# Shifting features by one token: transfers between partitions in place of products with 0/1 matrices

## The chip, the cores and the metric

The kernel runs on one core of one Trainium2 chip. The metric is the device time of one execution in microseconds (us), as the median of several runs. The core has five queues of work of its own that run side by side and wait for one another on semaphores: TensorE (PE, matrix products, its weight loads shown as PEld), VectorE (DVE), ScalarE (ACT), GpSimd (POOL) and SyncE (SP), which here only issues DMA transfers.

## The reference

The input x has 2 sequences of 1024 tokens with 128 features. Four blocks follow one another: a full attention with 16 heads, two layers of local attention with a feed-forward part, a causal attention with rotary positions, and a mixture of 8 experts; after each of them x plus the result is normalized. The change touches the two local layers. Cut to what matters:

```python
def shift_token(t):
    t1, t2 = jnp.split(t, 2, axis=-1)
    t2 = jnp.pad(t2, ((0, 0), (1, 0), (0, 0)))[:, :-1]
    return jnp.concatenate([t1, t2], axis=-1)

def _layer(x, wqkv, qs, ksc, wo, lg, lb, w1, b1, w2, b2):
    h = shift_token(x)
    q, k, v = jnp.split(h @ wqkv, 3, axis=-1)        # 8 heads of 64
    ...                                              # norm of q and k, rotation, windows of 64
    x = x + o @ wo
    h = shift_token(x)                               # the shift of this change
    h = (h - h.mean(-1)) / jnp.sqrt(h.var(-1) + 1e-05) * lg + lb
    a, g = jnp.split(h @ w1 + b1, 2, axis=-1)
    return x + (a * jax.nn.gelu(g, approximate=False)) @ w2 + b2
```

Features 64 to 127 of a token are replaced by those of the token before it in its sequence; the first token of a sequence gets zeros.

## The kernel before

Tokens lie on the 128 partitions. A sequence has 8 tiles of 128 tokens; 4 of them make a half, and a block is a (layer, sequence b, half hf). Within a block, token p of tile t lies on partition p at place t, so a shift by one token is a shift by one partition, and partition 0 of a tile needs what partition 127 of the tile before it holds.

The local layers run as one loop of 36 steps over 32 tiles (16 for each layer), written out by hand in `local_layers`. In a step each of some dozen stages works on another tile: the projection on the newest, scores two tiles behind it, the softmax three, the outputs four, the output projection five (`add_out`), and the sum that makes x1, the input of the feed-forward part, six behind (`add_x`, L813 on DVE, at the start of the step). Between the stages stand named places, `early`, `turns`, `mid`, `post` and `late`, into which the feed-forward pieces of a block are put by step number. PE, ACT, DVE and POOL do their work strictly in the order written. SP is not in that order: its transfers are placed by a planner at compile time.

The x1 of block k is complete with the `add_x` of step R = 4k + 9, for k from 0 to 6 the steps 9, 13, 17, 21, 25, 29 and 33. In that step, in the place `late` at its end:

- `ff_shift` (L461 to L474) has PE write the shifted half into a PSUM bank: a product with a 0/1 matrix that moves every row by one (L465), a second that carries the last row of a tile to the next (L466), and, for the second half of a sequence, one with the row kept from the first half (L468, tile `last`, made by POOL at L473).
- `ff_stats` (L476 to L481) builds the tile h: POOL copies the features that stay (L479), DVE copies the shifted ones out of PSUM (L480), and then `norm_factors` takes statistics on DVE (L99, L101) and a power on POOL (L105, L106).

One step later `ff_norm` applies the factors in place (L118 on DVE) and `ff_turn` transposes h for the products with w1. The PSUM bank comes from `single`, a pool of two banks that the loop's other small results share.

Around them, in step R, DVE has the scores of the step (L740, L745, L748), the division (L787, L789), and then, after the statistics, the next step's sums of squares (L689) and rotation (L696). POOL has the power of the query and key norms (L690, L691), the scaling (L701), the rotation's second half (L658, two products), and, for the next step, a copy of keys (L720), for which the score products on PE (L732) wait. For the blocks of layer 1 the sum with the local layers' input (`last_sum`: L545 on POOL, L99 on DVE, L105 and L106 on POOL) of block k-1 stands in `late` of the same step, ahead of `ff_stats`. SP issues two transfers in each step, of 64 partitions by 2080 bytes each, which copy values to other partitions (vh from vb, L680 and L683).

An eighth block, the last, is done by the same functions in the next attention's loop (`second_attention`).

Of the kernel before, what the change touches and what calls it, by code (L numbers as in the profile page):

```python
# [7 lines left out]
F32 = mybir.dt.float32  # L8
# [4 lines left out]
P = 128  # L13
B = 2
T = 1024
D = 128
NBLK = 2
NT = 4
# [29 lines left out]
def transformer_kernel(ctx: ExitStack, tc: tile.TileContext, a, out):  # L48
    nc = tc.nc
# [3 lines left out]
    xp = ctx.enter_context(tc.tile_pool(name="x", bufs=3))  # L53
# [36 lines left out]
    def norm_tiles(n):  # L90
        return (
            sp.tile([P, n, 6], F32, tag="ln_st", name="ln_st"),
            sp.tile([P, n, 2], F32, tag="ln_mv", name="ln_mv"),
            sp.tile([P, n], F32, tag="ln_rs", name="ln_rs"),
        )

    def norm_stats(y, tiles, which):
        for i in which:
            nc.vector.bn_stats(tiles[0][:, i, :], y[:, i, :])  # L99
        for i in which:  # L100
            nc.vector.bn_aggr(tiles[1][:, i, :], tiles[0][:, i, :])  # L101

    def norm_power(tiles, n):
        _, mv, rs = tiles
        nc.gpsimd.tensor_scalar_add(rs, mv[:, :, 1], EPS)  # L105
        nc.gpsimd.tensor_tensor(rs, rs, neghalf.to_broadcast([P, n]), ALU.pow)  # L106
        return mv, rs

    def norm_factors(y, n):

        tiles = norm_tiles(n)
        norm_stats(y, tiles, range(n))
        return norm_power(tiles, n)

    def norm_apply(o, y, factors, which):
        mv, rs = factors
        for i in which:
            nc.vector.tensor_scalar(  # L118
                o[:, i, :], y[:, i, :], mv[:, i, 0:1], rs[:, i : i + 1], ALU.subtract, ALU.mult
            )  # L120
# [333 lines left out]
    def feed_forward(pool2, single, double, ws, x1s, lasts, mbufs=1, gbufs=2):  # L454

        ffs = {}
        ones = [pool2.tile([P, 512], F32, name=f"mt2_{n}") for n in range(mbufs)]
        for mt in ones:
            nc.gpsimd.memset(mt, 1.0)

        def ff_shift(layer, b, hf):  # L461
            x1 = x1s[layer, b, hf]

            sh = single("ps_sh")[:, :256].rearrange("p (t d) -> p t d", d=64)
            nc.tensor.matmul(sh, shift, x1[:, :, 64:128], start=True, stop=False)  # L465
            nc.tensor.matmul(sh[:, 1:4, :], carry, x1[:, 0:3, 64:128], start=False, stop=(hf == 0))  # L466
            if hf:
                nc.tensor.matmul(  # L468
                    sh[:, 0, :], carry, lasts[layer, b], start=False, stop=True
                )  # L470
            else:
                lasts[layer, b] = xp.tile([P, 64], F32, tag="last", name="last", bufs=2)
                nc.gpsimd.tensor_copy(lasts[layer, b], x1[:, 3, 64:128])  # L473
            ffs[layer, b, hf] = {"sh": sh}  # L474

        def ff_stats(layer, b, hf):  # L476
            x1, sh = x1s[layer, b, hf], ffs[layer, b, hf]["sh"]
            h = pool2.tile([P, NT, D], F32, tag="h", name="h", bufs=2)
            nc.gpsimd.tensor_copy(h[:, :, 0:64], x1[:, :, 0:64])  # L479
            nc.vector.tensor_copy(h[:, :, 64:128], sh)  # L480
            ffs[layer, b, hf] = {"h": h, "ln": norm_factors(h, NT)}  # L481

        def ff_norm(layer, b, hf):
            f = ffs[layer, b, hf]
            norm_apply(f["h"], f["h"], f["ln"], range(NT))

        def ff_turn(layer, b, hf):
            f, w = ffs[layer, b, hf], ws[layer]
            ps = single("ps_hn")
            transpose_tiles(ps, lambda i: f["h"][:, i, :], NT)  # L490
            hnT = pool2.tile([P, 512], F32, tag="hnT", name="hnT", bufs=mbufs)
            nc.scalar.activation(hnT, ps, AF.Identity, scale=w["lng"], bias=w["lnb"])
            f["hnT"], f["mts"] = hnT, []

        def ff_in(layer, b, hf, c):
            f, w = ffs[layer, b, hf], ws[layer]
            c0, m = CH[c]
            ps = double("ps_w1")
            for n in range(2):
                nc.tensor.matmul(  # L500
                    ps[:m, n * 512 : (n + 1) * 512],
                    w["w1"][:, n * HID + c0 : n * HID + c0 + m], f["hnT"], start=True, stop=True,
                )
            gl = pool2.tile([P, 512], F32, tag="gl", name="gl", bufs=gbufs)
            nc.scalar.activation(gl[:m], ps[:m, 512:], AF.Gelu, bias=w["b1"][:m, 1, c : c + 1])
            f["parts"] = f.get("parts", {})
            f["parts"][c] = ps, gl

        def ff_gate(layer, b, hf, c):
            f, w = ffs[layer, b, hf], ws[layer]  # L510
            m = CH[c][1]
            ps, gl = f["parts"].pop(c)
            if c == 2:
                mt = ones[0]
                ones.append(ones.pop(0))
            else:
                mt = pool2.tile([P, 512], F32, tag=f"mt{c}", name=f"mt{c}", bufs=mbufs)
            nc.vector.scalar_tensor_tensor(  # L518
                mt[:m], ps[:m, :512], w["b1"][:m, 0, c : c + 1], gl[:m], ALU.add, ALU.mult
            )  # L520
            f["mts"].append(mt)

        def ff_out(layer, b, hf):
            f, w = ffs[layer, b, hf], ws[layer]
            ps = single("ps_w2")
            for i in range(NT):
                for c, (c0, m) in enumerate(CH):
                    m += c == 2
                    nc.tensor.matmul(
                        ps[:, i * P : (i + 1) * P], f["mts"][c][:m, i * P : (i + 1) * P],  # L530
                        w["w2"][:m, c, :], start=(c == 0), stop=(c == 2),
                    )
            f["ps"] = ps

        def ff_add(layer, b, hf):
            f = ffs.pop((layer, b, hf))
            x2 = xp.tile([P, NT, D], F32, tag=f"x{b}{hf}", name=f"xf_{b}{hf}")
            nc.vector.tensor_add(x2, f["ps"].rearrange("p (t d) -> p t d", d=D), x1s[layer, b, hf])
            x[b, hf] = x2

        return ff_shift, ff_stats, ff_norm, ff_turn, ff_in, ff_gate, ff_out, ff_add

    def last_sum(x_in, b, hf):
        y = xp.tile([P, NT, D], F32, tag="y", bufs=2, name=f"yl{b}{hf}")
# [18 lines left out]
    def local_layers(ws, tab):  # L563
# [20 lines left out]
        hTs, x1s, lasts, st = {}, {}, {}, [{} for _ in range(N)]  # L584
# [251 lines left out]
        early, turns, mid, post, late = {}, {}, {}, {}, {}  # L836

        def at(when, step, f, *args):
            when.setdefault(step, []).append((f, args))
# [9 lines left out]
        def steps(p, p2, ps, finish):  # L849
            nonlocal pool, pool2, psl  # L850
            pool, pool2, psl = p, p2, ps
# [6 lines left out]
                vbufs.append(v)  # L858
            for n in range(VH):
                vhbufs.append(pool.tile([P, 8, 65], F32, name=f"vh{n}"))  # L860
            ff_shift, ff_stats, ff_norm, ff_turn, ff_in, ff_gate, ff_out, ff_add = feed_forward(
                pool2, single, double, ws, x1s, lasts
            )

# [1 line left out]
            for k in range(7):  # L866
                block = layer, b, hf = k // 4, k % 2, k // 2 % 2
                ready = 4 * k + 9
                at(late, ready, ff_shift, *block)
                at(late, ready, ff_stats, *block)  # L870
                at(early, ready + 1, ff_norm, *block)
                at(late, ready + 1, ff_turn, *block)
                at(late, ready + 2, ff_in, *block, 0)
                at(early, ready + 3, ff_gate, *block, 0)
                at(turns, ready + 3, ff_in, *block, 1)
                at(mid, ready + 3, ff_gate, *block, 1)
                at(mid, ready + 3, ff_in, *block, 2)
                at(post, ready + 3, ff_gate, *block, 2)
                at(turns, ready + 4, ff_out, *block)
                at(mid, ready + 4, ff_add, *block)  # L880
                if layer == 0:
                    at(turns, ready + 5, next_head, 1, b, hf)
                else:
                    at(late, ready + 4, sum_up, b, hf)
                    if hf == 0:
                        at(early, ready + 5, lambda b, hf: normed[b, hf](), b, hf)
# [66 lines left out]
    def second_attention(pool, pool2, poolf, single, double, route, wc, woc, cs, ws, left):  # L953
# [133 lines left out]
        def group(f, g, *args):  # L1087
# [2 lines left out]


        norm_before, x_in, x1s, lasts = left
        ff_shift, ff_stats, ff_norm, ff_turn, ff_in, ff_gate, ff_out, ff_add = feed_forward(
            poolf, single, double, ws, x1s, lasts, mbufs=2, gbufs=4
        )
        early, late, normed = {}, {}, {}

        def at(when, step, f, *args):
            when.setdefault(step, []).append((f, args))
# [8 lines left out]
        block = (1, 1, 1)  # L1108
# [533 lines left out]
    with (  # L1642
# [8 lines left out]
        def single(name):  # L1651
            return psc.tile([P, 512], F32, tag="s", bufs=4, name=name)
# [99 lines left out]
```

## Time and profile before

| what | value |
|---|---|
| median of 3 runs | 1082.17 us (1081.94 to 1082.19) |
| the profiled execution | 1082.95 us, of which 1081.2 us are its span |
| busy: PE, DVE, ACT, POOL | 986.3, 797.5, 746.6, 569.9 us |
| first `add_x` of a complete block to the last (steps 9 to 33) | 514.2 us to 791.9 us from the span's start |
| a cycle of four steps in between | 45.7 to 46.8 us |
| granted TensorE clock, mean | 0.97 |

The busy time of an engine is an average over stages with quite different limits, so the stage is read by itself: the timeline of each engine within one step R, and what each instruction there waited for.

### The profile page before, as it was taken

How to read it: one execution, taken by the hardware profiler on the slowest of the kernel's cores; microseconds unless marked ns; L12 is line 12 of the kernel's file. 1: busy time of each engine (PE TensorE's matmuls, PEld its weight loads, DVE VectorE, ACT ScalarE, POOL GpSimd, SP SyncE). 2: the span in 40 equal slices, each digit the busy share in tenths (PEclk: the TensorE clock that was granted, in tenths of full speed). 3: DMA queues.
4: the chain of work that ended last, by engine and by line, in shares of the span. 5: the costliest groups of instructions: out<-in, count | busy, mean ns of one | idle time of the engine just before them, and what ended most of it. 6: DMA issues, size and time to landing. Idle time of an engine off the chain costs nothing. (4 is left out here: it accounts for less than half of the span.)

```text
span 1081.2 us, 21885 instructions
## 1 busy us (share of the span) xinstructions
PE 986.3 (91%) x8091; PEld 579.3 (54%) x8091; DVE 797.5 (74%) x1676; ACT 746.6 (69%) x1508; POOL 569.9 (53%) x625
## 2 busy tenths in 40 slices
PE   9999999999999999779989999999787799999891
PEld 3433333334333332456666757666564466689891
DVE  5988888887998887778968777695754387757443
ACT  1488888888888887568878788797662565444442
POOL 4044333434433433779978687786723135418653
PEclk8999999999999999889999999999898899999996
DMA  3111434112120200201101001010000000146883
GB/s 92 33 38 50 125 86 107 23 57 65 55 55 14 79 2 2 74 21 32 26 16 26 22 17 31 21 31 21 16 2 1 0 1 23 42 162 211 310 296 126
DMA packets 57211, 65.09 MB, mean 60 GB/s; under 512 B 9077, under 2 KB 43425, under 8 KB 57105
## 3 DMA queue, kind: packets, MB, share of 16 engines
q1 hardware_dynamic: 53472, 57.40, 18.2%
q0 software_dynamic: 2272, 4.92, 1.3%
q8 instruction: 64, 1.05, 0.4%
q10 hardware_dynamic: 1360, 1.38, 0.4%
q14 instruction: 43, 0.34, 0.1%
HBM read 37.98 MB, written 19.67 MB: 53 GB/s over the span
## 5 line engine op out<-in xcount | busy, mean ns | idle before, releaser
L232 DVE TENSOR_REDUCE mx<-s_max 128x1 f32<-128x512 f32 x512 | 318.5, 684 | 56.9 <-PE s_max L226 52.1
L263 ACT ACTIVATE pr<-s_exp 128x512 f32<-128x512 f32 x512 | 265.4, 603 | 64.4 <-PE s_max L226 49.0
L226 PE MATMUL s_max<-kTb,qm 32*128 32x512 f32 x1024 | 255.6, 624 | 0.5 <-DMA qm<-all 0.5
L282 POOL TENSOR_TENSOR av<-av,avp 128x512 f32<-128x512 f32 x101 | 128.0, 1267 | 239.5 <-ACT avp L281 221.6
L258 PE MATMUL s_exp<-q,kTb 32*128 32x512 f32 x1024 | 252.9, 616 | 0.0
L258 PEld LDWEIGHTS s_exp<-q,kTb 32*128 32x128 f32 x1024 | 101.8, 183 | 91.5 <-DVE mx L232 71.9
L270 PE MATMUL av<-pr,vp 128*32 128x512 f32 x1024 | 137.2, 605 | 0.7 <-ACT pr L263 0.7
L226 PEld LDWEIGHTS s_max<-kTb,qm 32*128 32x128 f32 x1024 | 104.4, 185 | 34.2 <-ACT pr L263 15.5
L756 ACT ACTIVATE pm<-pm,nb,rn 128x128 f32<-128x128 f32 x256 | 105.5, 490 | 0.1
L658 POOL TENSOR_TENSOR t<-raw,tab 128x512 f32<-128x512 f32 x64 | 86.1, 1367 | 19.4 <-DVE raw L626 10.8
L691 POOL TENSOR_TENSOR rn<-rn,neghalf 128x16 f32<-128x16 f32 x32 | 93.9, 2935 | 2.7
L650 DVE TENSOR_TENSOR t<-raw,tab 128x1024 f32<-128x1024 f32 x32 | 40.1, 1253 | 54.5 <-ACT raw L643 54.4
L270 PEld LDWEIGHTS av<-pr,vp 128*32 128x32 f32 x1024 | 20.6, 108 | 98.4 <-ACT pr L263 94.5
L281 ACT COPY avp<-av 128x512 f32<-128x512 f32 x101 | 60.1, 595 | 2.0 <-PE av L270 0.6
L637 PE MATMUL ps_qk<-wqkv,hT 128*128 128x512 f32 x120 | 58.7, 612 | 3.1 <-DVE o L789 2.5
L500 PE MATMUL ps_w<-hnT,w 128*128 128x512 f32 (+1 forms) x96 | 48.1, 632 | 12.9 <-DVE mt L518 9.6
L643 ACT COPY raw<-ps_qk 128x512 f32<-128x512 f32 x60 | 32.2, 589 | 37.9 <-PE ps_qk L637 37.2
L690 POOL TENSOR_SCALAR rn<-rn 128x16 f32<-128x16 f32 x32 | 31.2, 976 | 46.4 <-DVE rn L689 45.9
L1468 ACT ACTIVATE gj<-ps_fc 128x512 f32<-128x512 f32 x39 | 23.3, 597 | 41.1 <-PE ps_fc L1463 39.3
L1483 POOL DMA_INDIRECT yr<-yj,to x39 | 37.4, 958 | 23.8 <-DVE yj L1479 20.0
L689 DVE TENSOR_REDUCE rn<-sq 128x16 f32<-128x1024 f32 x32 | 38.7, 1209 | 9.7 <-ACT sq L665 9.6
L732 PEld LDWEIGHTS ps_sim<-kT,qT 64*64 64x64 f32 x1024 | 28.3, 135 | 31.9 <-issue 15.0
(232 smaller groups left out, 2009.6 us busy)
## 6 DMA issues: line engine op xcount, KB each, us to landing
wj<-ew SPq DMA_DIRECT2D x39, 512.0 KB
xs<-zero SPq DMA_DIRECT2D x8, 1152.0 KB
vh<-vb SPq DMA_DIRECT2D x60, 130.0 KB
xj<-xs SPq DMA_DIRECT2D x39, 72.0 KB
tab<-in_tab SPq DMA_DIRECT2D x2, 1024.0 KB
ew<-in_proj_w SPq DMA_DIRECT2D x8, 256.0 KB
ew<-in_fc_w SPq DMA_DIRECT2D x1, 2048.0 KB
wqkv<-in_wqkv SPq DMA_DIRECT2D x2, 768.0 KB
```

The source lines that it names most:

```text
L226: nc.tensor.matmul(s, q[32 * head : 32 * head + 32, qt * P : (qt + 1) * P], k[32 * head : 32 * head + 32, kh * 512 : (kh + 1) * 512], star ...
L232: return lambda: nc.vector.reduce_max(mx[:, head, qt, kh : kh + 1], s, axis=AX.X)
L258: nc.tensor.matmul(s, k[32 * head : 32 * head + 32, kt * P : (kt + 1) * P], q[32 * head : 32 * head + 32, :], start=True, stop=True,)
L263: return lambda: nc.scalar.activation(pr[:, head, :], s, AF.Exp)
L270: nc.tensor.matmul(ps[32 * h : 32 * h + 32, :], vps[m // 8][:, kt, 4 * g + h, :], pr[:, h, :], start=True, stop=True,)
L281: nc.scalar.copy(part, ps)
L282: nc.gpsimd.tensor_add(avs[m], avs[m], part)
L500: nc.tensor.matmul(ps[:m, n * 512 : (n + 1) * 512], w["w1"][:, n * HID + c0 : n * HID + c0 + m], f["hnT"], start=True, stop=True,)
L637: nc.tensor.matmul(ps[:, k * 512 : (k + 1) * 512], s["hT"], w["wqkv"][:, k * 512 : (k + 1) * 512], start=True, stop=True,)
L658: nc.gpsimd.tensor_mul(s["t2"][:, :, :, lo : lo + 32], raw4[:, :, :, hi : hi + 32], tabls[layer][:, t, 1, :, lo : lo + 32].unsqueeze(2).to ...
L691: nc.gpsimd.tensor_tensor(rn, rn, neghalf.to_broadcast([P, 16]), ALU.pow)
L756: nc.scalar.activation(s["pm"][:, k, :], s["pm"][:, k, :], AF.Exp, scale=s["rn"][:, head : head + 1], bias=s["nb"][:, k : k + 1],)
```

## The change

In the local layers' own loop the shift is done by DMA. A new function, `ff_move`, stands beside `ff_shift`; it is put in the place `early` of step R, right behind the `add_x` that completes x1. It allocates h, and SP issues two transfers or three: one of partitions 0 to 126 to partitions 1 to 127 (4 pieces of 64 numbers, 256 bytes, on each), one of partition 127's three pieces to partition 0 of the next tile, and for a second half one piece from the kept tile `last`. For a first half POOL fills that piece with zeros and makes `last`, as before. POOL's copy of the features that stay follows in the same place. `ff_stats`, still in `late` of step R, then finds h complete and begins with the statistics. The last block, in `second_attention`, keeps the products.

```diff
+        def ff_move(layer, b, hf):
+
+            x1 = x1s[layer, b, hf]
+            h = pool2.tile([P, NT, D], F32, tag="h", name="h", bufs=2)
+            nc.sync.dma_start(h[1:P, :, 64:128], x1[0 : P - 1, :, 64:128])
+            nc.sync.dma_start(h[0:1, 1:NT, 64:128], x1[P - 1 : P, 0 : NT - 1, 64:128])
+            if hf:
+                nc.sync.dma_start(h[0:1, 0, 64:128], lasts[layer, b][P - 1 : P, :])
+            else:
+                nc.gpsimd.memset(h[0:1, 0, 64:128], 0.0)
+                lasts[layer, b] = xp.tile([P, 64], F32, tag="last", name="last", bufs=2)
+                nc.gpsimd.tensor_copy(lasts[layer, b], x1[:, 3, 64:128])
+            nc.gpsimd.tensor_copy(h[:, :, 0:64], x1[:, :, 0:64])
+            ffs[layer, b, hf] = {"h": h}
+
         def ff_stats(layer, b, hf):
-            x1, sh = x1s[layer, b, hf], ffs[layer, b, hf]["sh"]
-            h = pool2.tile([P, NT, D], F32, tag="h", name="h", bufs=2)
-            nc.gpsimd.tensor_copy(h[:, :, 0:64], x1[:, :, 0:64])
-            nc.vector.tensor_copy(h[:, :, 64:128], sh)
-            ffs[layer, b, hf] = {"h": h, "ln": norm_factors(h, NT)}
+            f = ffs[layer, b, hf]
+            if "sh" in f:
+                x1 = x1s[layer, b, hf]
+                f["h"] = pool2.tile([P, NT, D], F32, tag="h", name="h", bufs=2)
+                nc.gpsimd.tensor_copy(f["h"][:, :, 0:64], x1[:, :, 0:64])
+                nc.vector.tensor_copy(f["h"][:, :, 64:128], f.pop("sh"))
+            f["ln"] = norm_factors(f["h"], NT)
...
                 ready = 4 * k + 9
-                at(late, ready, ff_shift, *block)
+                at(early, ready, ff_move, *block)
                 at(late, ready, ff_stats, *block)
```

The other lines of the diff pass both functions out of `feed_forward` and pick one of them in each loop.

## The prediction

> **What bounds the kernel now.** I read the shares first, only to drop them: they average over stages. Then the timeline of DVE through one step R (block 1, step 13), because the removed copy and the statistics are there; columns are start, length, engine, line, operation, and in brackets the idle time before it and its releaser.
>
> ```profile
> 559.93 0.29 DVE L813 TENSOR_TENSOR xl<-ps_wo,x 128x128 f32<-128x128 f32 x1
> 563.21 1.23 DVE L650 TENSOR_TENSOR t<-raw,tab 128x1024 f32<-128x1024 f32 x1 [2.99 <-ACT raw L643]
> ...
> 567.98 0.69 DVE L789 TENSOR_TENSOR o<-ps_o,rs 128x512 f32<-128x512 f32 x1
> 568.59 0.42 DVE L480 COPY h<-ps_sh 128x256 f32<-128x256 f32 x1
> 569.11 0.87 DVE L99 BATCH_NORM_STATS2 ln_st<-h 128x6 f32<-128x128 f32 x4
> 569.89 0.36 DVE L101 BATCH_NORM_AGGREGATE ln_mv<-ln_st 128x2 f32<-128x6 f32 x4
> 570.17 1.19 DVE L689 TENSOR_REDUCE rn<-sq 128x16 f32<-128x1024 f32 x1
> 571.28 1.22 DVE L696 TENSOR_TENSOR t<-t,t 128x1024 f32<-128x1024 f32 x1
> 572.41 0.28 DVE L813 TENSOR_TENSOR xl<-ps_wo,x 128x128 f32<-128x128 f32 x1
> ```
>
> From 563.21 DVE never stops, past the statistics into the next step. The same view later shows what it drives: its L789 at 579.07 frees the PSUM bank for which PE's projection waits (579.82), and its L518 at 590.74 releases PE's products with w1 (591.54), after which PE is continuous to the next step R. So what DVE loses or gains at L99 reaches the next block one for one. POOL is no bound there: it waited 2.03 us for L101 in this step. In step 9 POOL is nearly full, yet it too waits for L101 (1.28 us).
>
> Two more steps are different. Here DVE waits before L99 for POOL's copy, in step 9, and in steps 29 and 33, where that copy is queued behind the power of the other norm:
>
> ```profile
> 521.57 0.87 DVE L99 BATCH_NORM_STATS2 ln_st<-h 128x6 f32<-128x128 f32 x4 [0.59 <-POOL h L479]
> 757.36 0.87 DVE L99 BATCH_NORM_STATS2 ln_st<-h 128x6 f32<-128x128 f32 x4 [1.70 <-POOL h L479]
> 803.89 0.87 DVE L99 BATCH_NORM_STATS2 ln_st<-h 128x6 f32<-128x128 f32 x4 [1.52 <-POOL h L479]
> ```
>
> **What goes.** By the view of tile ps_sh: per block a product of 379 ns, one of 326 ns and for second halves one of about 247 ns on PE, some 0.7 to 0.95 us; none of it is on the path, since PE in step R+1 waits anyway for POOL's key copy (0.62 us at L732 in step 14, 1.81 us in step 10). The PSUM bank that goes frees the small pool; ps_sh waited for ACT's L678, and no other row shows that pool as what is short, so I take nothing. On DVE goes L480, 0.39 to 0.42 us: without it L99 could start at 568.59 instead of 569.11. The waits for POOL's copy go too, since that copy now runs early.
>
> **What moves.** POOL's copy (0.40 us) and, for first halves, the copy of the last row (0.23 us) go ahead of L658; with them a small memset (nearest row: L596, 64x1, 0.09 us). L658's results are needed only in the next step, and POOL's wait for L101 is longer than the 0.7 us: cost nothing in steps 9 to 25. Without that cover it would be 0.7 us a block. In step 29 there is no cover: POOL's sum L545 moves from 752.89 to some 753.6, and with it the other statistics on DVE, so that h's could start at about 756.1 rather than 755.3. The copies are disjoint from what the transfers write; L480 starting before L479 in step 33 (801.98 and 803.46) shows that such halves of h are not held apart.
>
> **What is added.** Up to three transfers on SP. Each costs SP about half a microsecond of issue (L683, L680: 0.46 and 0.55 us), and SP is idle most of each step; its vh transfers are due four steps later, so what queues behind costs nothing. The two small ones (3 pieces, 1 piece) resemble the copies of 4 rows (q from row), which land 1.7 us after issue. The long one decides. Its 127 x 4 pieces of 256 bytes go on as many DMA engines as what? The landing records of the trace tell: a transfer's semaphore takes one step for each engine used, the rest at once. The copies of 8 rows show 8 late steps, those of 64 or 128 rows 16, the load of 85 rows (part of w2, issued at 87.24) 5, with the other 11 credited 0.49 us after issue. The Trainium skill, page "DMA: Bandwidth & Descriptors", section "Why a DMA increments its semaphore by 16 and not by 1", has the rule: the largest number up to 16 that divides the slowest dimension, and it names 127 partitions as 1. The rows agree where there are any (85 = 5 x 17), and the rule speaks against this change: 508 pieces on one engine, not some 32 on each of 16.
>
> The stream's rate: the stores of zeros, 128 packets of 576 bytes on each engine, keep all engines full,
>
> ```profile
> core 0: us, PE busy (x) PEld busy (x) DVE busy (x) ACT busy (x) POOL busy (x), PEclk, DMA share, GB/s
> 90.00:94.00 4.00, 4.00 (x40) 1.40 (x34) 3.56 (x7) 3.62 (x8) 1.27 (x1) 1.00 1.02 294
> ```
>
> and the packet records show them back to back, first packet 1.0 us after issue and landing 0.35 us after the last. Packets of 256 bytes took 15 to 18 ns, and packets of 4 bytes on one engine follow each other every 18.7 ns though each took 7: so a piece costs the larger, 19 ns. The same page (section "Why small descriptors are slow (HBM only)") prices 256 bytes at 11 cycles, at the fabric clock it states (850 MHz) an estimate of 12.9 ns. Neither is an SBUF to SBUF row of this size; I take 19 ns as it is measured as a spacing, with 13 and 30 ns as ends (the 576-byte stores took 31).
>
> So h lands 0.05 (semaphore) + 1.0 + 508 x 0.019 + 0.35 = 11.05 us after x1 is complete:
>
> | step | x1 complete | h lands | DVE free for L99 | L99 before | change |
> |---|---|---|---|---|---|
> | 9 | 514.52 | 525.57 | 520.57 | 521.57 | +4.0 |
> | 13 | 560.22 | 571.27 | 568.59 | 569.11 | +2.2 |
> | 17 | 606.68 | 617.73 | 615.04 | 615.55 | +2.2 |
> | 21 | 652.75 | 663.80 | 661.13 | 661.65 | +2.1 |
> | 25 | 698.83 | 709.88 | 707.21 | 707.72 | +2.2 |
> | 29 | 745.36 | 756.41 | 756.1 | 757.36 | -0.9 |
> | 33 | 792.14 | 803.19 | 801.98 | 803.89 | -0.7 |
>
> Sum +11.0 us. Behind L99 in DVE's queue stand L101, L689, L696 and the next L813; for L101 waits POOL's L105, and behind that the key copy L720, for which PE's scores wait. The second effect is PE's clock. In step 29 PE already stands idle for L720, and the windows show what follows (PEclk is the third number from the end):
>
> ```profile
> 756.90:761.00 4.10, 0.00 (x0) 0.00 (x0) 3.64 (x12) 2.61 (x6) 2.74 (x5) 0.88 0.01 2
> 761.00:764.40 3.40, 3.35 (x44) 2.69 (x45) 3.40 (x10) 0.23 (x1) 3.23 (x2) 0.50 0.00 0
> 764.40:768.00 3.60, 3.60 (x38) 2.77 (x37) 3.22 (x6) 2.37 (x6) 3.52 (x4) 0.66 0.00 0
> ```
>
> There it costs DVE a wait of 1.39 us (L689, for ACT, for a slow ps_v). In step 9 the stall makes PE's idle time 1.8 + 4.0 + about 0.8 (the products gone), 6.6 us: I add 1.4 us. In steps 13 to 25 it comes to some 3.6 us, just under what the trace shows to suffice; I add nothing.
>
> Total +12.4 us against the profiled execution's 1082.95 us. The median of the runs stands 0.78 us below it; the same step gives 1082.17 + 12.4 = 1094.6 us.
>
> **Rivals.** *The transfer is in time* (forecast on the other side: faster). If it were spread on 16 engines, it would land some 2 us after x1, long before DVE comes: gains of 1.0, 4 x 0.52, 1.26 and 1.91 us, 6.2 in all, 1076 us. Nearly the same if pieces cost the page's 12.9 ns: landing after 8.0 us leaves +0.9 in step 9, then -4 x 0.52, -1.26, -1.91: -4.3, 1078 us. The point from which it decides is the landing at 8.4 us after x1 (DVE's arrival in steps 13 to 25), 13.8 ns a piece. For it: 15 ns packets are near. Against it: the 85-row record and the 18.7 ns spacing. Chance 0.13.
> *The transfer is just late*, 15 to 17 ns a piece: at 15 +2.0 + 0.4 - 1.3 - 1.9 = -0.8 us and at 17 +4.6, plus the clock in step 9: 1081 to 1088. Chance 0.12.
> *The forecast case*, 18 to 22 ns: 1089 to 1105. Chance 0.61.
> *Later still*: pieces of 25 to 30 ns (landing after 14 to 16.6 us: 32 to 50 us, and the clock drop in most blocks), or the planner puts the long transfer on SP behind vh's L683, which waits for ACT to 567.2 in step 13: it would land at about 578.3, 9.2 us later than L99 before, in five blocks, some +55 us with step 29. Against the latter: L680 is seen issued whenever its inputs are ready, and in steps as late as the one before. 1115 to 1145. Chance 0.14.
>
> **How the numbers follow.** The likeliest case gives 1094.6. The range runs from 1078 to 1125: it leaves out the spread transfer and the upper part of the last case. This kernel's measurement can tell some 0.2%, 2.2 us, from no change. Faster: the first rival, and little else, 0.13. Same: most of the second rival's lower end, 0.08. Slower: the rest, 0.79.
>
> **What would show it.** In the profile after: L99 waits for the DMA of h, 5 us in step 9 and 2.7 us in steps 13 to 25, shorter in 29 and 33; in the steps' windows one DMA engine busy for some 10 us; L465, L466 and L480 remain for the last block alone; the cycle of four steps 48 to 49 us in place of 45.7 to 46.8; PE's clock below 1 after step 9. Wrong would be: no wait for DMA at L99 (spread, or cheaper pieces), or a long transfer issued only after L678 (the planner).

## The result and the profile after

The kernel after takes 1100.34 us (median of 4 runs, 1098.78 to 1103.29) against 1082.18 us before: a ratio of 1.0163, 95% interval 1.0144 to 1.0181, slower by 18.2 us where 12.4 were forecast. The profiled execution took 1100.83 us, its span 1099.0 us.

The loss lies in the local layers' loop. From the start of its first `add_x` (step 6) to the start of its last (step 37) the profile before has 335.1 us and the profile after 352.4 us, 17.2 more. This stretch, called "the loop" below, is the finest measure there is: on every chip used here a step that is not touched repeats to some 0.1 us, but for steps 6 and 35. These two vary by up to 1.7 and 1.0 us, as a stretch of half PE clock does or does not fall into them (before and after have one in step 35, in ten of the other eleven profiles it is absent and the step 1.0 us shorter). Step n is counted from its `add_x` to the next.

The timeline of DVE after, in steps 9, 13 and 33, with the columns of the prediction (L830 is now `add_x`, L765 the product that makes nb, L806 the last work ahead of the statistics):

```profile
525.58 0.87 DVE L99 BATCH_NORM_STATS2 ln_st<-h 128x6 f32<-128x128 f32 x4 [5.01 <-DMA h<-xl]
...
565.78 0.28 DVE L830 TENSOR_TENSOR xl<-ps_wo,x 128x128 f32<-128x128 f32 x1
...
573.36 0.92 DVE L765 SCALAR_TENSOR_TENSOR nb<-nb,rn 128x8 f32<-128x8 f32 x1
...
574.43 0.69 DVE L806 TENSOR_TENSOR o<-ps_o,rs 128x512 f32<-128x512 f32 x1
576.80 0.87 DVE L99 BATCH_NORM_STATS2 ln_st<-h 128x6 f32<-128x128 f32 x4 [1.68 <-DMA h<-xl]
...
821.64 0.88 DVE L99 BATCH_NORM_STATS2 ln_st<-h 128x6 f32<-128x128 f32 x4 [0.43 <-DMA h<-xl]
```

The copy out of PSUM is gone, and in its place DVE waits for the transfer, 5.0 us in step 9 and 1.2 to 1.8 us in steps 13 to 25. The queue of SP in step 13, first column the issue, second how long SP was held (the one row from `last` is for the next block, due in step 17):

```profile
566.09 0.77 SPq L480 DMA_DIRECT2D h<-xl  x1
566.98 7.05 SPq L483 DMA_DIRECT2D h<-last  x1
574.14 0.53 SPq L700 DMA_DIRECT2D vh<-vb  x1
```

The long transfer is issued 0.03 us after x1 is complete, as early as can be. In the landing records its 508 packets run on one engine, from 1.41 to 9.67 us after issue, 16.3 ns each; 15 of the 16 completions are credited at once, the sixteenth comes at 10.61 us.

In the view of waits after, for DVE and for PE (total us, times, longest), PE's wait for POOL's keys is larger than DVE's for the transfer:

```profile
DVE ln_st L99 <- DMA h<-xl: 11.8, 6, 5.0
```

```profile
PE ps_sim L749 <- POOL kT L737: 16.1, 4, 6.9
PE ps_sim L749 <- POOL kT L739: 5.2, 2, 2.7
```

In the kernel before it was

```profile
PE ps_sim L732 <- POOL kT L720: 7.2, 4, 4.2
```

The scores of step 14, before and after:

```profile
572.80 1.10 PE L732 MATMUL ps_sim<-kT,qT 64*64 64x128 f32 x32 [0.62 <-POOL kT L720]
580.49 1.99 PE L749 MATMUL ps_sim<-kT,qT 64*64 64x128 f32 x32 [3.34 <-POOL kT L737]
```

What the wait sets off is seen in the windows of steps 14 and 20 after (stretch and length, then the busy us of PE, PEld, DVE, ACT and POOL with their instructions; PEclk is the third number from the end):

```profile
577.30:580.50 3.20, 0.01 (x1) 0.01 (x2) 3.20 (x10) 2.56 (x6) 2.32 (x3) 0.89 0.01 3
580.50:583.50 3.00, 3.00 (x38) 2.34 (x38) 2.92 (x7) 0.00 (x0) 2.89 (x2) 0.50 0.00 0
648.80:650.70 1.90, 0.00 (x0) 0.00 (x0) 1.88 (x3) 1.84 (x3) 1.82 (x2) 1.00 0.00 0
650.70:653.70 3.00, 2.97 (x5) 1.22 (x6) 0.00 (x0) 0.00 (x0) 2.92 (x2) 0.62 0.01 3
```

PE idles 3.3 us in step 14, for keys, and only 1.96 us in step 20, for DVE, and each time its next products run at about half speed: in step 14 the scores take 1.99 us instead of 1.10. While they crawl ACT has nothing to do (0.00 in the window), so the loss is handed to it and, it seems, from it to DVE; the runs with idle products below test that. The chain of waits gives the transfer itself 5% of the span:

```profile
PE s_exp L258 13%; PE av L270 11%; PE s_max L226 10%; DMA h<-xl 5%; PE ps_w L517 3%; PE ps_qk L654 3%; POOL yr L1500 2%; PE ps_sc L1030 2%; PE ps_oc L1071 2%; ACT pm L773 2%; DVE rn L706 2%; DVE mx L232 2%; DVE t L713 1%; DVE pm L757 1%; DVE nb L762 1%
```

That is not the price of the change. The chain counts whole transfers (5% are some 55 us, five landings of 10 to 11 us), and most of each lies beside work that was there before. Step by step, after less before, in us:

| steps | change |
|---|---|
| 9, 13, 17, 21, 25 (the waits) | +3.45, +1.84, +1.71, +1.58, +1.38 |
| 29, 33 | -1.51, -1.41 |
| the steps behind: 10, 11, 14, 15, 19, 23, 27 | +0.80, +1.02, +1.35, +1.23, +1.13, +1.16, +1.24 |
| 20, 24 | +1.70, +1.70 |
| 30 | -1.21 |

The steps with the waits sum to +7.0, those between to +10.1. So there were two questions for the experiments: does the long transfer wait because it is on one engine, and does the larger half come from PE's clock or from the delay itself?

### The profile page after: what moved, and what is told of

Read it like the earlier page. It is cut to its first block, busy times and chain, and to the rows that moved or that the text cites. A ratio compares the mean times of both kernels' runs of the same rounds, so it can differ in the third digit from the quotient of the medians.

```text
span 1099.0 us, 21860 instructions
## 1 busy us (share of the span) xinstructions
PE 991.4 (90%) x8057; PEld 582.2 (53%) x8057; DVE 797.7 (73%) x1669; ACT 747.1 (68%) x1508; POOL 569.8 (52%) x629
## 3 DMA queue, kind: packets, MB, share of 16 engines
q10 hardware_dynamic: 1360, 1.38, 0.4%
## 4 chain that ended last, share of the span: by engine, by line
PE 59%; DVE 16%; POOL 7%; ACT 7%; DMA 6%; issue 3%; ACTq 0%; POOLq 0%; SPq 0%; DVEq 0%
PE s_exp L258 13%; PE av L270 11%; PE s_max L226 10%; DMA h<-xl 5%; PE ps_w L517 3%; PE ps_qk L654 3%; POOL yr L1500 2%; PE ps_sc L1030 2%; PE ps_oc L1071 2%; ACT pm L773 2%; DVE rn L706 2%; DVE mx L232 2%; DVE t L713 1%; DVE pm L757 1%; DVE nb L762 1%
## 5 line engine op out<-in xcount | busy, mean ns | idle before, releaser
L654 PE MATMUL ps_qk<-wqkv,hT 128*128 128x512 f32 x120 | 60.9, 632 | 3.5 <-DVE o L806 3.1
L749 PE MATMUL ps_sim<-kT,qT 64*64 64x128 f32 x1024 | 38.4, 292 | 21.3 <-POOL kT L737 16.1
```

The costliest lines, as they stand in the source:

```text
L654: nc.tensor.matmul(ps[:, k * 512 : (k + 1) * 512], s["hT"], w["wqkv"][:, k * 512 : (k + 1) * 512], start=True, stop=True,)
L749: nc.tensor.matmul(psv[64 * win : 64 * win + 64, r, c, :], s["qT"][64 * r : 64 * r + 64, c, 64 * win : 64 * win + 64], s["kT"][64 * r : 64 ...
```

## The experiments

The runs were made on three chips. On the first two (two groups of four kernels) the kernel before took 1092.7 us, on the third 1082.5. In the profiles made there, what differs is behind the loop: from the last `add_x` to the end 268.7 to 270.6 us on the first two, against 260.2 to 262.2 on the third and in the shown profiles. Why the chips differ there was not looked for. Of the kernel before there is only the shown profile, and behind the loop two executions on one chip can differ by some 2 us, so a ratio and a loop need not agree to better than that. So times are compared as ratios to the kernel before on the same chip, and steps by the loop.

| kernel | ratio to before (95%) | loop, us |
|---|---|---|
| before (shown profile) | 1 | 335.1 |
| after (shown profile) | 1.0163 (1.0144 to 1.0181) | 352.4 |
| after_again | 1.0145 (1.0123 to 1.0166) | 350.8 |
| split113 | 1.0028 (1.0015 to 1.0041) | 338.6 |
| split112 | 0.9925 (0.9913 to 0.9937) | 329.8 |
| warm1 | 1.0138 (1.0123 to 1.0154) | 349.5 |
| warm2 | 1.0040 (1.0020 to 1.0060) | 336.9 |
| warm23 | 1.0041 (1.0028 to 1.0054) | 340.3 |
| keep_early | 0.9980 (0.9968 to 0.9992) | 332.8 |
| split112_fill | 0.9942 (0.9927 to 0.9957) | 329.7 |
| split112_late | 0.9936 (0.9917 to 0.9955) | 326.7 |
| products_best | 0.9945 (0.9925 to 0.9965) | 326.2 |
| best | 0.9905 (0.9887 to 0.9923) | 323.9 |

**split112: the same transfer, cut so that it divides.**

```diff
-            nc.sync.dma_start(h[1:P, :, 64:128], x1[0 : P - 1, :, 64:128])
+            nc.sync.dma_start(h[1:113, :, 64:128], x1[0:112, :, 64:128])
+            nc.sync.dma_start(h[113:P, :, 64:128], x1[112 : P - 1, :, 64:128])
```

> The kernel after with the long transfer cut in two, 112 rows (16 x 7) and 15 rows, nothing else changed. Theory (127 rows sit on one engine, and that is the whole loss): both land some 2 us after x1 is complete, no wait for a DMA is left at the statistics (L100 in this numbering), the scores in the next step wait 2.5 us less for POOL's key copy, and the clock drops behind the blocks go: 1074 to 1079 us, some 6 us under the kernel before. Rival (the route by DMA itself is slow: its start, pieces of 256 bytes, SP's order): the statistics still wait for the DMA, 1090 to 1100 us. Second rival (landing cured, but the loss in the steps behind comes from something else): no wait at the statistics and still over 1084 us.

112 rows land 2.3 to 2.4 us after issue (2.9 once), with 16 late completions; the 15 rows 2.2 us after theirs, with 15. DVE in step 13, and SP:

```profile
567.84 0.91 DVE L766 SCALAR_TENSOR_TENSOR nb<-nb,rn 128x8 f32<-128x8 f32 x1
568.67 0.20 DVE L805 RECIPROCAL rs<-ps_o 128x8 f32<-128x8 f32 x1
568.90 0.69 DVE L807 TENSOR_TENSOR o<-ps_o,rs 128x512 f32<-128x512 f32 x1
569.51 0.86 DVE L99 BATCH_NORM_STATS2 ln_st<-h 128x6 f32<-128x128 f32 x4
```

```profile
560.56 0.67 SPq L480 DMA_DIRECT2D h<-xl  x1
561.29 0.94 SPq L481 DMA_DIRECT2D h<-xl  x1
562.34 0.60 SPq L484 DMA_DIRECT2D h<-last  x1
```

No bracket at L99: it no longer waits, and SP is not held. The steps between (10 to 12, 14 to 16 and so on to 28) are back at their old lengths or 0.1 us under, but for step 12 (+1.69, below). The ratio is 0.9925, some 8 us under before, where 6 were expected; the loop is 5.3 us shorter, 1.0 of it in step 35. The theory holds, the rivals fall. Two things were not as thought. Steps 13, 17, 21 and 25 change by only -0.18 to +0.08 us against before, where the 0.5 us of the copy out of PSUM should show; and nb takes 0.91 us in place of 0.31.

**split113: a dose.** Same edit with 113 and 14 rows.

> The kernel after with the long transfer cut into 113 rows (a prime) and 14 rows: a dose. Theory (the largest number up to 16 that divides the rows sets the engines): the 113 rows stay on one engine, 452 pieces x 16.3 ns instead of 508, so they land 0.9 us earlier, some 9.5 us after x1; the statistics wait 0.9 us less in each of steps 9 to 25 (0.3 to 1.0 us left in 13 to 25, 4.1 us in step 9). If each us at the statistics costs one us, and the slow clock behind them stays: 1095 to 1097 us. Rival A (it is the size of the transfer, not the divisor: 113 rows spread on all engines): lands after 2 us, 1074 to 1080 us. Rival B (the wait at the statistics does not carry on one for one): 1099 to 1101 us.

```profile
573.20 0.87 DVE L99 BATCH_NORM_STATS2 ln_st<-h 128x6 f32<-128x128 f32 x4 [0.70 <-DMA h<-xl]
```

```profile
563.45 0.79 SPq L480 DMA_DIRECT2D h<-xl  x1
564.30 6.04 SPq L481 DMA_DIRECT2D h<-xl  x1
```

113 rows stay on one engine: one late completion, landing 9.2 to 9.4 us after issue, and SP is held 6 us by the transfer behind it. So the divisor decides, not the size. The wait in step 13 falls from 1.68 to 0.70 us, as the theory said. But the time does not: the ratio of 1.0028 is 1085.2 us on the scale of 1082.2, ten less than expected, and the loop is 13.8 us shorter than in the kernel after. The steps with the waits give 4.7 of these, 0.5 to 1.0 us a step as the dose says; of the other 9.1 us, 7.8 come from the steps behind, 10 to 28, and 1.0 from step 35. In steps 18, 19, 22, 23, 26 and 27 nothing is lost any more, and PE's idle time ahead of the scores there is 1.6 to 2.3 us with no half clock, where the kernel after has 2.5 to 2.9.

**keep_early: POOL's copy alone.** The kernel before, its products kept; POOL's copy L479 is put at the start of step R.

> The kernel before, with the products kept; only POOL's copy of the features that stay is moved to the start of step R, as in the kernel after. Theory (the waits of DVE for that copy, 0.59, 1.70 and 1.52 us in steps 9, 29 and 33, are what the change gains, and DVE hands it on one for one): these waits go, but in step 29 POOL's sum comes 0.4 us later: -2.5 to -3.5 us, 1078.5 to 1079.7 us. Rival (the wait is taken over by another, for the shifted half out of PE or for POOL's power): within 1 us of the kernel before. Rival (0.4 us more ahead of the rotation's second half on POOL costs in steps 13 to 25): slower than before, 1083 to 1085 us.

The ratio is 0.9980, 2.2 us, a little less than the theory said; the loop is 2.4 us shorter, with step 12 at +1.69 and step 35 at -1.02 in it, both by PE's clock. Steps 9, 29, 30 and 33 gain 0.14, 1.31, 1.09 and 1.49 us. But each of steps 13, 17, 21, 25 is 0.32 to 0.36 us longer, which the last rival said. In this kernel's step 13, DVE and POOL:

```profile
569.74 0.66 DVE L754 SCALAR_TENSOR_TENSOR nb<-nb,rn 128x8 f32<-128x8 f32 x1
...
569.09 1.29 POOL L664 TENSOR_TENSOR t<-raw,tab 128x512 f32<-128x512 f32 x1
```

and in the kernel before:

```profile
567.52 0.31 DVE L748 SCALAR_TENSOR_TENSOR nb<-nb,rn 128x8 f32<-128x8 f32 x1
...
566.53 1.27 POOL L658 TENSOR_TENSOR t<-raw,tab 128x512 f32<-128x512 f32 x1
```

nb has two SBUF operands and 8 elements a partition. It ends when POOL's rotation ends, at 570.4 here and 567.8 before (start and length added up), and in split112 too, where it is longest; the copy that moved ahead on POOL pushes the rotation back, and DVE's small product stretches with it. With nothing on POOL beside it, it is shorter still, as in step 12 of the kernel before:

```profile
554.35 0.17 DVE L748 SCALAR_TENSOR_TENSOR nb<-nb,rn 128x8 f32<-128x8 f32 x1
```

**warm1: a fill that was too long.** PE gets idle products ahead of the scores, to keep its clock.

```diff
             psv = ps.rearrange("p (r c k) -> p r c k", r=2, k=P)
+            if n in (8, 12, 16, 20, 24):
+                for i in range(12 if n == 8 else 6):
+                    nc.tensor.matmul(
+                        ps[:, :512], ident, ws[0]["w1"][:, :512], start=True, stop=True
+                    )
```

> The kernel after, its transfers as they are; PE gets products that nothing reads (6 of 128x128 by 512, 12 in step 10) ahead of the scores in steps 10, 14, 18, 22 and 26, into the bank that the scores overwrite, in the time in which it waits for POOL's key copy (2.7 to 3.4 us, 6.9 in step 10). Clock theory (PE's idle time there halves its clock, and the slow products make the next two steps 0.8 to 1.35 us longer each): the clock stays at 1.00 in steps 14, 15, 18, 19, 22, 23, 26, 27; these steps lose 6 to 8 us, to 1092 to 1095 us. Rival (the delay of DVE and POOL is handed on, whatever the clock): 1099 to 1102 us, the clock at 1.00 or not.

The clock stayed at 1.00 from 484 to 778 us, and still the steps lost: 1.0138. PE in step 14:

```profile
575.81 5.31 PE L748 MATMUL ps_sim<-w,cst 128*128 128x512 f32 x12
...
581.05 1.10 PE L754 MATMUL ps_sim<-kT,qT 64*64 64x128 f32 x32
```

As a test of the clock this fails. Each such product in float32 takes PE 0.88 us (two rows of the view), not the 0.44 I had reckoned, so in step 14 the six held PE for 5.3 us, and the scores started at 581.05 though their keys were there at 579.20. The fill put a delay in the place of the slow clock, and one thing can be learned from it: steps 11, 15, 19, 23 and 27 lost 1.02 to 1.24 us, each what it lost in the kernel after (to 0.01 us), though the clock was at full. What is handed on is that PE ends its scores late, whether a slow clock or a fill made them late.

**warm2, warm23, after_again: the fill at its right length.** 6, 3, 2, 2 and 2 products in steps 10, 14, 18, 22 and 26; in warm23 one more in steps R + 3. The kernel after, unchanged, was run on the same chip.

> The kernel after, unchanged, on the chip of the experiments, where the kernel before took some 1092 us in the first group of runs, 10 us more than in the shown runs, all of it behind the last add_x of the local layers. Theory: from the first add_x to the last, 352.4 us as in the shown profile (352.4 against 335.1 before), the ratio to the kernel before 1.015 to 1.018. Rival: the loop differs with the chip too, by more than 2 us.

> The kernel after, its transfers as they are, with half the idle products of the first try, which overran the wait by 0.6 to 1.8 us and so took the place of what they were to save: 6 products of 128x128 by 512 ahead of the scores of step 10, 3 in step 14, 2 in steps 18, 22 and 26 (0.88 us each, for waits of 6.9, 3.3, 2.7, 2.5 and 2.9 us). Nothing reads them. Clock theory (a grid window of 3.41 us in which PE is busy for less than some 45% is followed by one at half clock, and this makes the steps behind R longer): no half clock behind steps 10 to 26, steps 10, 11, 14, 15, 19, 23 and 27 lose 0.8 to 1.35 us each, 7.5 us together, the loop 344 to 346 us, less another 1.7 to 3.4 if steps 20 and 24 come to lie elsewhere on the grid; ratio 1.006 to 1.010. Rival (it is the lateness of the scores itself that carries on through ACT and POOL, at any clock): the loop stays at 350 to 353 us, ratio 1.014 to 1.018, although the clock is 1.00.

> As warm2, and one such product more (0.88 us, into a small bank that nothing reads) in steps 12, 16, 20, 24, 28, where PE waits 1.8 to 2.0 us for DVE's gate ahead of the second products with w1. Clock theory: these waits alone bring a window under 45% busy when they lie whole in one window of the grid; with the product none does, so no step R + 3 is 1.7 us longer: the loop 340.5 to 344.5 us, that is the 335.1 of before, plus the 7.0 us of the waits for the transfer, plus up to 1.5 where a fill ends late; ratio 1.005 to 1.008. Rival: as for warm2, 350 us or more.

after_again repeats the shown profile within 0.2 us in every step from 7 to 34. warm2 in step 14:

```profile
573.20:576.70 3.50, 2.78 (x7) 0.95 (x5) 3.50 (x12) 2.61 (x6) 2.32 (x3) 1.00 0.01 2
576.70:579.70 3.00, 2.99 (x69) 2.59 (x70) 2.92 (x7) 1.21 (x3) 2.88 (x2) 1.00 0.03 5
```

The scores follow at full clock, 69 products in 3 us where the kernel after did 38. Its transfers and the waits for them are those of the kernel after (steps 9 to 25: +3.44, +1.81, +1.69, +1.53, +1.44), yet every step between, 10 to 12, 14 to 16, 18 to 20, 22 to 24, 26 to 28, is back at the length of before or 0.1 us under it. In step 14 the scores begin 0.39 us after `add_x` in before, after and warm2 alike, and end 1.50, 2.38 and 1.50 us after it: only the slow clock makes them late. So the 11.3 us that these steps had lost were PE's clock, all of them, and the rival (the delay carries on by itself) is out. Nor does SP's 7 us behind the long transfer cost anything: it is there in warm2 too. The loop came out at 336.9 us, below the 344 to 346 expected: steps 20 and 24 were cured as well (3.4 us), steps 6 and 35 fell 1.6 and 1.0 us shorter on the grid, and steps 29 to 31 together 1.0 us shorter than in the kernel after. In warm23 step 6 and steps 29 to 31 were not shorter (340.3), and its extra products changed nothing in steps 12 to 28, where nothing was left for them to cure: its expectation is met, but not for its reason.

**The clock over all thirteen profiles.** The clock's records change at multiples of 3.413 us only. For each such window from 500 to 822 us at full clock I took the share in which PE was busy, and the clock of the window that follows:

| PE busy in the window | windows | next one at half |
|---|---|---|
| below 0.42 | 24 | 24 |
| 0.42 to 0.47 | 10 | 5 |
| above 0.47 | 1157 | 1 |

So it is not the length of one idle time that counts but how it falls on the grid: 1.96 us in step 20 within one window (0.43 busy) suffice, 2.26 us over two (split113, step 26) do not. In step 12 PE waits 2.0 us in the kernel before, in split112 and in keep_early alike; the window was 0.43 busy before, and the clock stayed, 0.40 in the other two, and it fell: +1.69 us.

**split112_fill: is step 12 that?** The cut, and one idle product in each step R + 3.

```diff
+            if c == 1 and (layer, b, hf) != (1, 1, 1):
+                nc.tensor.matmul(
+                    single("warm"), ident, ws[0]["w1"][:, :512], start=True, stop=True
+                )
             ps = double("ps_w1")
```

> The transfer cut into 112 and 15 rows, with the one idle product in each step R + 3. In the run with the cut alone one step (12) was 1.7 us longer than before although PE's wait in it was the same 2.0 us: there 60% of a grid window was idle and the next one ran at half clock, while in the kernel before it was 57% and it did not. Clock theory: the product takes that away, step 12 is back at 15.84 us, the loop 328.1 us against 329.8 with the cut alone, ratio 0.990 to 0.992. Rival (the 1.7 us are from something else, or the product stands in the way of the gate's products): step 12 stays at 17.5 us or every step R + 3 is longer by up to 0.3 us, ratio 0.9925 or more.

Step 12 is back at 15.84 us. Two other steps took the gain away, 30 (+1.2 us against split112; the clock at half there for 6.8 us) and 36 (+0.86, the same kind of product there), so the loop is 329.7 and the ratio 0.9942, not the expected one. The reading of step 12 holds; the sum did not.

**split112_late: the long nb.** POOL's copy goes back to the end of steps 13 to 25 and stays early in steps 9, 29 and 33.

> The transfer cut into 112 and 15 rows; POOL's copy of the features that stay goes back to the end of the step for blocks 1 to 4 (steps 13, 17, 21, 25) and stays early in steps 9, 29 and 33. Port theory (DVE's small product of two SBUF operands, nb from nb and rn, cannot run beside POOL's rotation, which the early copies push 0.4 to 0.9 us later; it took 0.31 us before, 0.66 us with the copy alone moved, 0.91 us in step 13 of the cut transfer, and ended each time just when POOL's product ended): nb is back at some 0.3 to 0.5 us and steps 13, 17, 21, 25 are 0.3 to 0.5 us shorter each than with the cut alone (12.0 to 12.2 us), the loop 1.2 to 2 us shorter than 329.8 us, apart from a step of 1.7 us that the clock may add or take. Rival (nb is long for its own reason, and DVE then waits for POOL's late copy instead): steps unchanged at 12.3 to 12.6 us, a wait for POOL's copy at the statistics.

nb takes 0.58, 0.32, 0.32 and 0.93 us in steps 13, 17, 21, 25 (0.91, 0.67, 0.66, 0.91 with the cut alone), and the first three steps are 0.33 to 0.35 us shorter than there. Step 25 is not: there POOL still ran its memset and the copy of the last row ahead of the rotation, which ended at 703.86, POOL's copy followed without a gap until 704.20, and nb, begun at 703.30, ended at 704.23. (In best, where nb began a little earlier against them, it took 0.56 us and the step was 0.36 us shorter.) No wait for POOL appears at the statistics. The port theory holds. The ratio does not show it (0.9936, against 0.9925 with the cut alone): the loop is 3.1 us shorter than there, 1.7 of it step 12, but this is another chip, and the profile is 2.0 us longer than before's behind the loop.

**best and products_best: what the transfer is worth.** best is split112_late with idle products in steps 10, 14, 26 (one), 30 (two), 12, 16, 20 and 28 (one). products_best is the kernel before with POOL's copy early in steps 9, 29, 33 and the two idle products in step 30.

> As split112_late, with idle products that nothing reads in PE's waits: one in steps 10, 14 and 26 and two in step 30 ahead of the scores, one in steps 12, 16, 20 and 28 ahead of the second products with w1. Theory: no window of the clock's grid is idle enough up to step 32, so steps 30 and 31 fall to some 9.2 and 8.9 us as in warm2 (10.7 and 10.4 before), and no step R + 3 gains 1.7 us: the loop 324 to 326.5 us, ratio to before 0.988 to 0.992, below the cut alone (0.9925). Rival (the gains of the clock in steps 29 to 31 are handed back to another wait before step 37): the loop 327 to 329 us.

> The kernel before with its products with 0/1 matrices kept, and the two repairs that have nothing to do with transfers: POOL's copy early in steps 9, 29 and 33 alone, and two idle products on PE in step 30. This is what the transfer has to be compared with. Theory: steps 9, 29 and 33 gain 0.1, 0.8 to 1.3 and 1.5 us, steps 30 and 31 2 to 3 us, steps 13 to 25 nothing: the loop 329.5 to 331.5 us, ratio 0.994 to 0.997; what is left to the transfer, the copy out of PSUM (0.4 to 0.5 us in seven blocks) and the earlier start in step 9, is 4 to 5 us against the kernel called best. Rival (the transfer's gain is only that of POOL's copy and of the clock): within 1.5 us of the kernel called best.

best has a ratio of 0.9905 and a loop of 323.9 us, the clock at 1.00 from 487 to 821 us; steps 30 and 31 take 9.20 and 8.59 us. products_best: 0.9945 and 326.2, under the 329.5 to 331.5 expected; 1.5 us are a step 6 shorter by the clock's grid, which best had not, and 1.0 is step 35, which both had. On the same chip the medians stand 4.5 us apart (1072.47 and 1076.99), so the kernel with the transfer, well cut, is some 4 us of the 10 faster; the other 6 are POOL's copy and PE's clock, to be had with the products too. Of these 4 about 1.0 is not the transfer either: nb takes 1.29 us in step 9 of products_best and 0.31 in best, where POOL also makes `last` early. That order could be had with the products; it was not tried.

## Why the prediction was right, and where it was not

The direction was right, and the cause named for it, the transfer on one engine, stands behind both halves of the loss: with the transfer cut both are gone. That the sum came as near as it did is in part luck, because two errors have opposite signs: the landing was forecast to cost 4.0 us more than it did, PE's clock 8.7 us less.

- *DVE hands on one for one* (from 563.21 it never stops): right in steps R. In split113 the wait of step 13 fell by 0.98 us and the step by 0.97.
- *One engine*: right, and it carries the verdict. Page "DMA: Bandwidth & Descriptors" of the Trainium skill, section "Why a DMA increments its semaphore by 16 and not by 1", gives the rule of the divisor; the rows here agree for 127, 113, 112 and 15 rows (1, 1, 16 and 15 late completions).
- *19 ns a piece*: too much, as 12.9 was too little. It was 16.3 ns, with a first packet at 1.4 us (not 1.0) and the landing 0.6 to 0.9 us behind the last (not 0.35): 10.2 to 10.6 us after issue instead of 11.0. That lies between the forecast and the rival "just late", whose 15 to 17 ns were the right rate, but with the early first packet put the landing at 9.0 to 10.0 us.
- *L99 per step*, +11.0 us in all: the steps R sum to +7.0. The statistics begin 10.3 to 10.7 us after x1 is complete, where 11.05 was forecast, and that is the whole of the difference.
- *The moved POOL copies cost nothing*: the reason given, POOL's own slack, failed. In steps 13 to 25 they cost DVE 0.3 to 0.6 us a block through nb (in step 9 they save 0.6: 0.94 us before, 0.31 after). In the kernel after this only shortens the wait for the transfer, which ends later anyway; once the transfer is spread it is what is left.
- *PE's clock, +1.4 us in step 9 alone*: the term that was mis-sized, and the main error. It is 11.3 us, in seven steps after a wait for POOL and two after a wait for DVE, less 1.2 us in step 30, whose stretch of half clock is 3.4 us instead of 6.8. The step that failed is "in steps 13 to 25 it comes to some 3.6 us, just under what the trace shows to suffice": I compared the length of one idle time with one seen before, where the share of a grid window decides, and 57% of 3.413 us, some 1.95 us, are already enough. Page "TensorE: Matmul & The Clock Gate", section "Part 1: The HAM clock gate", knows the free-running window of 3413 ns but names a whole idle window as what drops the clock; the measured table decides, and less does it.
- *No wait put in PE's place by the products that go*: right (L465, L466 and the copy remain for the last block alone). *vh and SP*: right that it costs nothing, though SP was held 7 us, not half a microsecond.
- *The planner's rival*: did not occur. It issued the long transfer at once, and the three-piece one a step early.
- *What would show it*: the wait in step 9 was named as 5 us and is 5.01; 2.7 us in steps 13 to 25 were 1.2 to 1.8. The cycle of four steps, forecast as 48 to 49 us, is 50.5 to 51.0 us for the cycles that start at steps 9 to 21, by the clock.

## What to carry to other kernels

Cut a transfer between partitions so that its slowest count has a large divisor up to 16: 112 and 15 rows instead of 127 turn a landing of 10.3 us into two of 2.3. Before a stall is priced by its own length, look at what PE does in it: here the windows of 3.413 us of the clock's grid in which PE was busy for less than some 45% cost a second time, 11.3 us against 10.0 for the waits in steps 9 to 25 themselves, and products that nothing reads, no longer than the wait, took that away. And compare a new way with the old one after both have had the repairs that have nothing to do with it.

## Of the hardware, not expected

- A single row of 256 bytes (h from `last`) went out as 16 pieces of 16 bytes, one on each engine. Behind the full engine SP was held 7.05 us at its issue and it landed after 9.9 us; with the cut SP was held 0.60 us and it landed after 1.8 us.
- DVE's product of 8 elements a partition with two SBUF operands (nb) stands 328 times between 505 and 800 us of the thirteen profiles. 104 of them took 0.17 to 0.18 us. Each of the other 224, of 0.19 to 2.16 us, ended 0.02 to 0.03 us after one of POOL's instructions (in step 13 of before, keep_early and split112: 567.83 and 567.80, 570.40 and 570.38, 568.75 and 568.72 us). The longest, in step 29 of split112 and of warm2, sat out two of them in a row. The Trainium skill, page "SBUF — State Buffer", section "Terms", names the port pair that the two share, and that the loser blocks; DVE's neighbours with an operand in PSUM or with one input kept their length.
- In a window at half clock PE must be busy for more than some 80% for the next to be at full (29 of 29 above that share, none of 8 below it, in the same windows of the thirteen profiles).
